# Reducing 32 keys per tile in two more groups of a position-bias network, and a pair in the last one

## The chip, the cores and the metric

The kernel runs on one core of a Trainium2 chip. The metric is device time in microseconds (us) for one launch, taken as the median over several runs. In the listings PE is the matrix engine, PEld its weight loads, DVE the vector engine, ACT the scalar (activation) engine, POOL the GpSimd engine and SP the engine that only issues transfers. POOL and SP both issue DMA transfers here: SP plain copies, POOL copies that add to what lies at the destination.

## The reference, cut to what matters

The input is `x`, two images of 512 channels and 32 x 32 pixels. Layer 0 is an attention block with deformable keys: 8 heads per image give 16 groups, and each group has 1024 queries (the pixels) and 64 keys (sampled positions). Most of the work is a small network that turns every query-key offset into one bias:

```
pos = grid_q[:, :, None, :] - grid_kv[:, None, :, :]
bias = sign(pos) * log1p(abs(pos))
bias = relu(bias @ cpb_w1 + cpb_b1)      # 2 -> 128
bias = relu(bias @ cpb_w2 + cpb_b2)      # 128 -> 128
bias = bias @ cpb_w3 + cpb_b3            # 128 -> 1
sim = q @ k + bias;  attn = softmax(sim);  out = attn @ v
```

The attention's output goes through `out_w` and is added to `x`; then comes an MLP of 512, 2048 and 512 channels. Layer 1 is ordinary attention over the 1024 pixels with four 512 x 512 projections. Everything is float32.

## The kernel before, in words

**Slots.** The bias network runs in one long loop over 256 slots, `for s in range(NS)`. A slot is 4 keys against all 1024 queries, and 16 slots make a group (`NSL = 16`, `NG = 16`). For each slot DVE builds the first hidden layer `h1` in one custom instruction (`st_layer1`, line 678), two slots ahead and into three buffers. PE multiplies it by the second weights in four quarters `z` of 32 hidden channels each (`st_layer2`, line 695). The four keys lie in four groups of 32 output partitions, so a result is 128 partitions (4 keys x 32 channels) x 1024 queries. ACT applies bias and relu (lines 708 and 710).

**Summing channels without PE.** The third layer is a weighted sum over 128 channels. The kernel sums quarters 0 and 1, and 2 and 3, with two DVE instructions (`st_sum`, line 718). A POOL transfer then adds the second sum to the first (line 720). What is left is `sums[s][1]`: 4 keys x 32 partial channels. Then transfers between partitions shrink it, in levels. A *fold* adds half of a tile's rows to the other half (16 partial channels per key). A *copy* puts the free half of the rows of the next tile beside it, and a *join* adds the other half of that tile. After this one tile carries twice as many keys with half as many rows each. Level 1 makes tiles of 8 keys out of pairs of slots, level 2 tiles of 16 keys out of four slots, level 3 tiles of 32 keys out of eight. Folds and joins are POOL transfers (`add`, line 737), copies are SP transfers (`move`, line 744). `LEVELS` (line 785) lists each level's step, the slot at which it ends, its three moves and how many slots after the tile's first slot each is due; `LAST` (line 790) shortens these delays in the last group. `due` collects them, and each slot issues what is due. `add` chains the POOL transfers with `issue_after`, so POOL's queue has a fixed order, and an instruction that waits holds all that is behind it.

**The projection.** `st_layer3` (line 800) multiplies a group's finished tiles by mask weights (`w3f`, `w3u`), which sum the remaining rows of every key. They are made on POOL in `arrange` from columns of the constant `mask`. Each product writes 32 rows of the group's scores `sim` in PSUM: row block `64 h + 32 i`, with `h` the half of the queries and `i` the half of the group's keys. The products accumulate onto q times k (line 809). `FULL = NS - 3 * NSL = 208` says where level 3 ends: groups 0 to 12 have two tiles of 32 keys and 4 products, issued 27 slots after the group's start. Groups 13 and 14 have four tiles of 16 keys and 8 products, issued 22 slots after it (line 934). Group 15, the last, has three tiles of 16 keys. Slots 252 to 255 stand alone, each with its own product (weights `w3u`), and slot 255 has one more for its second sum: 16 products in all, after the loop.

**Softmax and what follows.** `softmax_steps` (line 836) is a generator: ACT takes `sim` out of PSUM, PE transposes it, DVE takes maxima, ACT exponentiates in eight parts and scales, and for every second group PE transposes back (`pb`, line 880). The loop runs one step per slot in most slots. What is left over runs after the loop. There `project(0, ...)` starts the output projection (PE, line 1029); between its products it runs three steps of the last group's softmax at a time.

**Buffers around it.** The first sum of a slot takes a buffer by its place among eight: `u8` (4 buffers), `uo` (3), `uc` (2), and `u4` (2) for place 4. Tile `x6` is a fifth kind, used for slots 228 and 252 in place of `u4` (line 705). After the loop it serves as the fourth block sum that the projection needs, written there by the last `spread` (lines 945 and 946). The other sums of these blocks, `spread` 0 to 2 and `fold` 0 to 3 on `op0`, are done by DVE in the loop, one every fourth slot after slot `ready`.

Of the kernel before, what the change touches and what calls it, by code (L numbers as in the profile page):

```python
# [8 lines left out]
F32 = mybir.dt.float32  # L9
# [48 lines left out]
def conv_seq_kernel(ctx: ExitStack, tc: tile.TileContext, x, xt, kst, pst, cst, vec, wsm, outw, w1, w2, wl, wlt, brow, out):  # L58
# [25 lines left out]
    w3f = cp.tile([P, 80], F32, name="w3f")  # L84
    w3u = cp.tile([P, 60], F32, name="w3u")
    for w in (w3f, w3u):
        nc.gpsimd.memset(w, 0.0)
# [103 lines left out]
    def op_blocks(b, parts, wsum):  # L191
        v, q = vp[:, b * NCH : b * NCH + NCH, :], qa[:, b]
        w = [v[:, k : k + 2, n : n + 256] for k, n in ((0, 0), (2, 0), (2, 256), (0, 256))]
        x = [q[:, k : k + 2, n : n + 512] for k in (0, 2) for n in (0, 512)]
        return w + [wsum[:, j] for j in range(3)], x + [parts[:, j] for j in range(parts.shape[1])]

# [10 lines left out]
    with tc.tile_pool(name="lp", bufs=2) as lp:  # L207
# [32 lines left out]
        nc.gpsimd.dma_start(out=cs, in_=cst)  # L240
        nc.gpsimd.dma_start(out=pz[:, 0:437], in_=pst)
        nc.gpsimd.dma_start(out=ident, in_=kst)

        def load(b, k, wq=None):
# [20 lines left out]
        w2t, crow, tri, chan, mask = (  # L265
            pz[:, a:b] for a, b in ((0, 128), (128, 256), (256, 384), (384, 385), (385, 437))
        )
# [26 lines left out]
        def arrange():  # L294
# [18 lines left out]
            nc.gpsimd.tensor_scalar(w3f[:, 48:64], mask[:, 32:48], sc[:, 8:9], None, ALU.mult)  # L313
            nc.gpsimd.tensor_scalar(w3u[:, 28:32], mask[:, 48:52], sc[:, 8:9], None, ALU.mult)

        state = {}
# [371 lines left out]
        def st_layer2(s):  # L688
            h1 = h1s.pop(s)
            r = []  # L690
            for z in range(4):
# [10 lines left out]
                )[z]  # L702
                pool = lp
                if z == 1 and s % 8 == 4 and s >= FULL and (s - FULL) // 8 % 3 == 2:
                    pool, name, bufs = op, "x6", 1
                o = pool.tile([P, 2, 512], F32, name=name, bufs=bufs)
                if z % 2 == 0:
# [72 lines left out]
        def st_join3(s):  # L780
            for o, i in zip(fours(s, 1), fours(s + 4, 0)):
                add(o, i)

        FULL = NS - 3 * NSL
        LEVELS = (
            (8, FULL, (st_copy3, st_join3, st_fold3), (14, 15, 11)),
            (4, NS - 4, (st_copy2, st_join2, st_fold2), (7, 8, 6)),
            (2, NS - 4, (st_copy, st_join, st_fold), (3, 4, 2)),
        )
# [10 lines left out]
        def st_layer3(s):  # L800
# [17 lines left out]
            if s + NSL == NS:  # L818

                w = [w3u[:, 12 - 4 * o : 44 - 4 * o] for o in range(4)]  # L820
                parts[1][1:] = [(w[o], sums[s + 12 + o][1]) for o in range(4)] + [(w[3], sums[s + 15][3])]
                parts[0] = 4 * [None] + parts[0]
            for m in range(len(parts[1])):
# [69 lines left out]
        for s in range(NS):  # L893
# [19 lines left out]
            if bg is not None and state.get(len(CHAINS) - 1, 0) is None:  # L913

                bg = None
                php.__exit__(None, None, None)
                opp = tc.tile_pool(name="op", bufs=1, side="right")
                op = opp.__enter__()
                op0 = op_blocks(
                    0, op.tile([P, 2, 2, 512], F32, name="op0x"), op.tile([P, 3, 2, 256], F32, name="op0w")  # L920
                )
                ready = s
            if bg is None and s > ready and (s - ready) % 4 == 0 and (s - ready) // 4 <= 7:
                i = (s - ready) // 4 - 1
                if i < 3:
                    spread(op0[1], (i,))
                else:
                    fold(nc.vector, op0[0], which=(i - 3,))

# [14 lines left out]
        next(tail)  # L944
        op0[1].append(op.tile([P, 2, 512], F32, name="x6", bufs=1))
        spread(op0[1], (3,))

# [556 lines left out]
def _order(np):  # L1504
# [9 lines left out]
    alone = (d // 32)[:, None] == np.arange(4)  # L1514
    return np.concatenate([crow, tri, d[:, None], eight, four, alone], axis=1).astype(np.float32)

# [87 lines left out]
```

## Time and profile before

| what | value |
|---|---|
| median of 3 runs | 2612.42 us (2611.72 to 2614.12) |
| the profiled execution's own time | 2612.25 us |
| its span, first to last instruction | 2610.5 us |
| PE busy, in matmuls | 2597.5 us, 19660 instructions |
| DVE busy | 2303.7 us |
| ACT busy | 1754.3 us |
| POOL busy | 980.6 us |
| second-layer products (line 695) | 1772.0 us, 16384 instructions |
| projection products (line 828) | 168 instructions |
| mean busy share of the DMA engines in the loop | mostly 0.8 to 0.9 in the page's 40 slices |

The span is what the profiler sees, and 1.75 us of the execution lie outside it. A float32 product appears as two PE instructions, so a slot's 32 products are 64. Matmuls overlap, so a group's busy time is read from the start times of its rows. A row of the timeline merges neighbours of one kind: start, duration, engine, line, operation, operands, count. The program's names have lost their numbers, so `u` stands for `u8` and `u4`, and `x` for `x6`.

### The profile page before, as it was taken

To read this page: it belongs to the slowest core of one execution; us is meant where nothing else is said; L and a number is where in the kernel's file an instruction comes from. 1 tells how busy PE (TensorE), PEld (TensorE's weight loads), DVE (VectorE), ACT (ScalarE), POOL (GpSimd) and SP (SyncE) were. 2 spreads that over 40 slices of the span, in tenths; PEclk is the share of its full clock that TensorE was granted. 3 is DMA by queue.
4 is the path that set the end of the run, shared out by engine and by line. 5 is a ranking of instruction groups with operands and counts; after the bars stand their busy time and mean duration, and the time that the engine had idled before them with its cause. 6 is when DMAs were issued, how large, how long until landed. Compare 5 with 4: busy or idle time off the path is not lost.

```text
span 2610.5 us, 49004 instructions
## 1 busy us (share of the span) xinstructions
PE 2597.5 (100%) x19660; PEld 1009.8 (39%) x19660; DVE 2303.7 (88%) x1459; ACT 1754.3 (67%) x2362; POOL 980.6 (38%) x1122
## 2 busy tenths in 40 slices
PE   9999999999999999999999999999999999999999
PEld 3332333333233233223333333332355655646656
DVE  6999999999999999999999999999776587666656
ACT  5887888888888888888788777777733242314041
POOL 1344444444444444444454444333322334200100
PEclk9999999999999999999999999999999999999999
DMA  5889999999998999899999899888777768400202
GB/s 187 173 192 197 194 194 195 195 189 191 200 191 189 188 204 203 175 191 202 191 197 192 186 193 193 176 174 186 153 200 171 147 148 167 91 16 1 73 1 56
DMA packets 177634, 428.27 MB, mean 164 GB/s; under 512 B 30048, under 2 KB 78320, under 8 KB 174720
## 3 DMA queue, kind: packets, MB, share of 16 engines
q0 software_dynamic: 107392, 273.09, 58.4%
q1 hardware_dynamic: 69584, 151.75, 17.5%
q8 instruction: 155, 2.54, 0.4%
q14 instruction: 71, 0.58, 0.1%
q10 hardware_dynamic: 432, 0.31, 0.0%
HBM read 82.16 MB, written 6.55 MB: 34 GB/s over the span
## 4 chain that ended last, share of the span: by engine, by line
PE 96%; DVE 3%; ACT 1%; issue 0%; DMA 0%; DVEq 0%; ACTq 0%
PE ps L695 67%; PE sw L1082 7%; PE sw L1253 7%; PE sw L160 7%; PE sw L1029 2%; PE sw L1351 2%; PE psg L597 1%; PE sim L828 1%; DVE hm L137 1%; PE psx L1329 1%; PE sim L809 0%; PE pt L845 0%; PE pkv L534 0%; PE pb L880 0%; PE psq L333 0%
## 5 line engine op out<-in xcount | busy, mean ns | idle before, releaser
L695 PE MATMUL ps<-h,cw 128*32 128x512 f32 x16384 | 1772.0, 592 | 1.8 <-ACT rx L708 1.0
L678 DVE CUSTOM_DVE_ANT_1 h<-ta,tb 128x4096 f32<-128x4096 f32 (+1 forms) x257 | 1131.3, 4402 | 28.9 <-PE ps L695 24.0
L695 PEld LDWEIGHTS ps<-h,cw 128*32 128x32 f32 x16384 | 527.7, 110 | 1214.0 <-issue 1160.4
L708 ACT ACTIVATE rx<-ps,sc 128x1024 f32<-128x1024 f32 x512 | 568.6, 1111 | 138.4 <-PE ps L695 115.5
L737 POOL DMA_DIRECT2D u<-u x394 | 406.9, 1514 | 2.5 <-issue 2.2
L710 ACT ACTIVATE ub<-ps,sc 128x1024 f32<-128x1024 f32 x256 | 308.4, 1205 | 90.6 <-PE ps L695 90.5
L720 POOL DMA_DIRECT2D uo<-ub x127 | 111.4, 877 | 600.1 <-DVE ub L718 570.0
L718 DVE SCALAR_TENSOR_TENSOR ub<-rx,sc,ub 128x1024 f32<-128x1024 f32 x256 | 327.3, 1278 | 3.1 <-ACT ub L710 3.1
L1082 PE MATMUL sw<-hm,w2t 128*128 128x512 f32 x448 | 194.0, 592 | 0.2 <-DVE hm L125 0.2
L710 ACT ACTIVATE uo<-ps,sc 128x1024 f32<-128x1024 f32 x128 | 154.3, 1205 | 43.9 <-PE ps L695 40.7
L718 DVE SCALAR_TENSOR_TENSOR uo<-rx,sc,uo 128x1024 f32<-128x1024 f32 x128 | 163.7, 1279 | 7.6 <-ACT uo L710 7.0
L737 POOL DMA_DIRECT2D u<-uc x124 | 124.8, 1280 | 17.6 <-DMA u<-uc 15.3
L1082 PEld LDWEIGHTS sw<-hm,w2t 128*128 128x128 f32 x448 | 84.9, 190 | 104.0 <-issue 97.9
L720 POOL DMA_DIRECT2D uc<-ub x64 | 55.4, 866 | 179.9 <-DVE ub L718 147.9
L137 DVE TENSOR_TENSOR hm<-hm,sw 128x512 f32<-128x512 f32 x79 | 57.6, 732 | 73.0 <-PE sw L160 50.6
L720 POOL DMA_DIRECT2D u<-ub x62 | 53.1, 856 | 178.8 <-DVE ub L718 178.8
L737 POOL DMA_DIRECT2D uc<-uc x63 | 107.6, 1708 | 0.0
L737 POOL DMA_DIRECT2D uc<-uo x63 | 102.8, 1632 | 10.6 <-DMA uc<-uo 10.3
L1417 POOL DMA_DIRECT2D xs<-rs x6 | 7.2, 1200 | 259.6 <-DVE rs L137 259.6
L737 POOL DMA_DIRECT2D u<-uo x62 | 84.8, 1368 | 21.6 <-DMA u<-uo 18.4
L658 ACT ACTIVATE ta<-fb,vs 128x512 f32<-128x512 f32 (+1 forms) x65 | 89.1, 1374 | 5.6 <-DMA fb<-fdr 5.6
L710 ACT ACTIVATE uc<-ps,sc 128x1024 f32<-128x1024 f32 x64 | 77.0, 1203 | 21.2 <-PE ps L695 19.3
(306 smaller groups left out, 2648.2 us busy)
## 6 DMA issues: line engine op xcount, KB each, us to landing
uo<-ub POOLq DMA_DIRECT2D x127, 512.0 KB, 5.4
fb<-fdr SPq DMA_DIRECT2D x64, 512.0 KB, 5.7
uc<-ub POOLq DMA_DIRECT2D x64, 512.0 KB, 6.0
u<-ub POOLq DMA_DIRECT2D x62, 512.0 KB, 6.3
uc<-uc POOLq DMA_DIRECT2D x63, 256.0 KB, 8.3
uc<-uo SPq DMA_DIRECT2D x63, 256.0 KB, 3.2
uc<-uo POOLq DMA_DIRECT2D x63, 256.0 KB, 5.7
u<-u POOLq DMA_DIRECT2D x62, 256.0 KB, 6.9
```

Of the source, the lines that this page charges most:

```text
L137: nc.vector.tensor_tensor(out, a, b_, op)
L160: nc.tensor.matmul(bank[:, e, :], w, x, start=(q in (1, 2, 5) and e == k == 0), stop=True, skip_group_check=True,)
L658: nc.scalar.activation(ta.rearrange("p j x -> p x j")[:, :, j0:j1], fb[:, 0, :, j0:j1], AF.Identity, bias=col("cb1"), scale=col("w1x"),)
L678: nc.vector._custom_dve(TENSOR_ADD_SAT, out=h1[:, y : y + step].rearrange("p y t x -> p (y t x)"), in0=a.unsqueeze(1).to_broadcast([P, ste ...
L695: nc.tensor.matmul(ps[32 * q : 32 * q + 32, h, :], cw2[:, 32 * z : 32 * z + 32], h1[:, 16 * h : 16 * h + 16, q, :], start=True, stop=True,)
L708: nc.scalar.activation(o, ps, AF.Relu, bias=sc[:, 4 + z : 5 + z])
L710: nc.scalar.activation(o, ps, AF.Relu, bias=sc[:, 4 + z : 5 + z], scale=sc[:, z : z + 1])
L718: nc.vector.scalar_tensor_tensor(r[1], r[0], sc[:, z : z + 1], r[1], ALU.mult, ALU.add)
L720: nc.gpsimd.dma_start(out=sums[s][1], in_=sums[s][3], accum_op=ALU.add)
L737: nc.gpsimd.dma_start(out=out, in_=in_, accum_op=ALU.add)
L1082: nc.tensor.matmul(ps[:, m, :], w[:, a, k, m * P : (m + 1) * P], x[:, b_, k, :], start=(k == 0), stop=(k == 1),)
L1253: nc.tensor.matmul(ps[:, m, :], w[:, a, k, c + m * P : c + (m + 1) * P], x[b_][:, k, :], start=(k == 0), stop=(k == nk - 1),)
```

## The change

`FULL` moves from slot 208 to slot 240, so that groups 13 and 14 reduce to tiles of 32 keys and are projected like groups 0 to 12, and only the last group keeps tiles of 16 keys. Level 1 now ends at slot 254 instead of 252: slots 252 and 253 are folded, copied and joined as a pair, with mask weights of their own (`w3p`, from 8 new columns of the constant). `x6` goes away. Every slot of place 4 takes `u4`, the projection's fourth block sum gets its place in `op0x`, and its `spread` moves into the loop, ahead of the folds, which come four slots later each.

```diff
-    w3u = cp.tile([P, 60], F32, name="w3u")
-    for w in (w3f, w3u):
+    w3u = cp.tile([P, 36], F32, name="w3u")
+    w3p = cp.tile([P, 32], F32, name="w3p")
+    for w in (w3f, w3u, w3p):
         nc.gpsimd.memset(w, 0.0)
...
+            nc.gpsimd.tensor_scalar(w3p[:, 16:24], mask[:, 52:60], sc[:, 8:9], None, ALU.mult)
...
-                pool = lp
-                if z == 1 and s % 8 == 4 and s >= FULL and (s - FULL) // 8 % 3 == 2:
-                    pool, name, bufs = op, "x6", 1
-                o = pool.tile([P, 2, 512], F32, name=name, bufs=bufs)
+                o = lp.tile([P, 2, 512], F32, name=name, bufs=bufs)
...
-        FULL = NS - 3 * NSL
+        FULL = NS - NSL
         LEVELS = (
             (8, FULL, (st_copy3, st_join3, st_fold3), (14, 15, 11)),
             (4, NS - 4, (st_copy2, st_join2, st_fold2), (7, 8, 6)),
-            (2, NS - 4, (st_copy, st_join, st_fold), (3, 4, 2)),
+            (2, NS - 2, (st_copy, st_join, st_fold), (3, 4, 2)),
         )
...
-                w = [w3u[:, 12 - 4 * o : 44 - 4 * o] for o in range(4)]
-                parts[1][1:] = [(w[o], sums[s + 12 + o][1]) for o in range(4)] + [(w[3], sums[s + 15][3])]
-                parts[0] = 4 * [None] + parts[0]
+                w = [w3u[:, 4 - 4 * o : 36 - 4 * o] for o in range(2)]
+                parts[1][1:] = [(w3p, sums[s + 12][1])] + [(w[o], sums[s + 14 + o][1]) for o in range(2)]
+                parts[1].append((w[1], sums[s + 15][3]))
+                parts[0] = 3 * [None] + parts[0]
...
-                    0, op.tile([P, 2, 2, 512], F32, name="op0x"), op.tile([P, 3, 2, 256], F32, name="op0w")
+                    0, op.tile([P, 3, 2, 512], F32, name="op0x"), op.tile([P, 3, 2, 256], F32, name="op0w")
...
-            if bg is None and s > ready and (s - ready) % 4 == 0 and (s - ready) // 4 <= 7:
+            if bg is None and s > ready and (s - ready) % 4 == 0 and (s - ready) // 4 <= 8:
                 i = (s - ready) // 4 - 1
-                if i < 3:
+                if i < 4:
                     spread(op0[1], (i,))
                 else:
-                    fold(nc.vector, op0[0], which=(i - 3,))
+                    fold(nc.vector, op0[0], which=(i - 4,))
...
-        op0[1].append(op.tile([P, 2, 512], F32, name="x6", bufs=1))
-        spread(op0[1], (3,))
...
+    two = (4 * (d % 2) + d // 32)[:, None] == np.arange(8)
-    return np.concatenate([crow, tri, d[:, None], eight, four, alone], axis=1).astype(np.float32)
+    return np.concatenate([crow, tri, d[:, None], eight, four, alone, two], axis=1).astype(np.float32)
```

More of the change, by code (lines that the diff above doesn't have):

```diff
@@ L194, in op_blocks @@
         x = [q[:, k : k + 2, n : n + 512] for k in (0, 2) for n in (0, 512)]
-        return w + [wsum[:, j] for j in range(3)], x + [parts[:, j] for j in range(parts.shape[1])]
+        return w + [wsum[:, j] for j in range(3)], x + [parts[:, j] for j in range(3)]
     zp = ctx.enter_context(tc.tile_pool(name="zp", bufs=3, space=PSUM))
@@ L240, in conv_seq_kernel @@
         nc.gpsimd.dma_start(out=cs, in_=cst)
-        nc.gpsimd.dma_start(out=pz[:, 0:437], in_=pst)
+        nc.gpsimd.dma_start(out=pz[:, 0:445], in_=pst)
         nc.gpsimd.dma_start(out=ident, in_=kst)
@@ L265, in conv_seq_kernel @@
         w2t, crow, tri, chan, mask = (
-            pz[:, a:b] for a, b in ((0, 128), (128, 256), (256, 384), (384, 385), (385, 437))
+            pz[:, a:b] for a, b in ((0, 128), (128, 256), (256, 384), (384, 385), (385, 445))
         )
```

## The prediction

> **What bounds the kernel now.** I read the page's first part, then the chain of work that ended last, in order of time.
>
> ```profile
> PE 2597.5 (100%) x19660; PEld 1009.8 (39%) x19660; DVE 2303.7 (88%) x1459; ACT 1754.3 (67%) x2362; POOL 980.6 (38%) x1122
> 1511.69 0.86 PE sim L828 x8
> 1624.16 1.00 PE sim L828 x8
> 1701.85 1.72 PE sim L828 x16
> 1815.90 1.85 PE sim L828 x16
> 1881.44 4.29 PE sim L828 x25
> ```
>
> From 1480 us to the loop's end the chain never leaves PE, and a slot's 64 matmuls take 6.87 us. So PE sets the end, and every product removed from it is time, unless something makes PE wait. The five rows are the projections of groups 11, 12 (two tiles of 32 keys), 13, 14 (four tiles of 16) and 15.
>
> Next, the timeline of PE at the loop's end, and that of POOL, whose queue feeds it:
>
> ```profile
> 1881.26 1.04 PE L828 MATMUL sim<-u,w3f 128*32 128x512 f32 x4
> 1882.12 1.04 PE L828 MATMUL sim<-x,w3u 128*32 128x512 f32 x4
> 1882.98 0.61 PE L828 MATMUL sim<-uo,w3u 128*32 128x512 f32 x2
> 1885.66 1.13 PE L1029 MATMUL sw<-qa,vp 128*128 128x512 f32 x2
> 1901.12 1.04 PE L880 MATMUL pb<-ident,sx 128*128 128x128 f32 x8
> ```
>
> ```profile
> 1866.10 0.88 POOL L720 DMA_DIRECT2D x<-ub  x1 [3.42 <-DVE ub L718]
> 1868.17 0.84 POOL L737 DMA_DIRECT2D uc<-uo  x1 [1.20 <-DMA uc<-uo]
> 1869.86 0.88 POOL L720 DMA_DIRECT2D uo<-ub  x1 [0.85 <-DVE ub L718]
> 1870.43 1.16 POOL L737 DMA_DIRECT2D u<-uc  x1
> 1877.06 0.82 POOL L737 DMA_DIRECT2D u<-uc  x1 [5.47 <-DMA u<-uc]
> 1877.60 1.17 POOL L720 DMA_DIRECT2D uc<-ub  x1
> ```
>
> PE goes from the last slot into the last projection with no gap: slot 252's own sum (`x`) was started at 1866.10 and is used at 1882.12. The DMA view of these moments gives issue to landing: 5.8 us for `x<-ub` (512 KB), 5.7 for `uo<-ub`, 4.9 for `uc<-uo` (256 KB), 4.8 for the last `uc<-ub`.
>
> [...] 16 instructions over all four row blocks take 1.72 us, while a tile of the last group that fills only two blocks takes 0.86 us for 4 (1882.12 to 1882.98), twice as much each. [...] POOL stood 5.47 us before the join at 1877.06, with slot 254's sum behind it.
>
> **The change part by part**, against the profiled execution (2612.25 us: span 2610.5 and 1.75 around it, 0.17 below the median 2612.42).
>
> 1. Groups 13 and 14 lose four products each. By the chain's rows: 1.72 - 0.86 and 1.85 - 1.00, so -1.71 us, all on PE's path.
> 2. Group 15 loses one two-block tile (two products): -0.86.
> 3. Pair 252/253, the wait added. It is worked out in the clock of before, as both sides move together with PE. The fold can start when 252's sum has landed, 1866.10 + 5.8 = 1871.9. In POOL's new order it stands behind 253's sum and ahead of the first `u<-uc`. It lands behind 253's sum (1875.6), with the 4.9 of a 256 KB row at about 1876.8. The copy then goes out on SP, which is free; SP's copy at 1865.32 let POOL go on at 1868.17, 2.85 us, so 1879.7. The join is last in POOL's queue, behind 254's sum: 1879.7 + 4.9 = 1884.6. PE comes to the pair's product at 1882.12, the second of its order, and everything behind it on PE waits too: the other tiles, the transposes and the projection. **+2.5 us.** Bounds: with the fastest 256 KB landing near the end (4.2) for fold and join the sum is there at 1883.2 (+1.1). With 5.7 for both and 4.85 for the copy (SP 1810.33 to POOL 1815.18) it is 1888.2 (+6.1). I take the middle rows, which carry the load of this moment.
> 4. Softmax of group 14. Its projection moves from 22 to 27 slots after the group's start, group 13's from 230 to 235, and group 13's steps (one more now) fill the slots to 255. So all of group 14's softmax but the read of `sim` falls after the loop; before, all of it but the last scalings was done there. The PE transposes only move (0.59). But ACT now has eight exponentials (2.6 us, as at 1894.11 to 1896.8), eight scalings (2.0) and a copy (0.58) in front of the last group's. It reached these at 1894.11, 6.3 us after taking `sim` at 1887.83. In the new order the first maxima also stand behind the 1.23 us block sum that waits for the last projection. Adding up, `sim` taken at S lets group 14's exponentials end at S+4.2, the projection's copy at 5.2, scalings at 7.2, copy 7.8, maxima 9, exponentials 11.7, then a reciprocal queued behind two PSUM sums, scalings done near S+15. PE reaches `pb` 13.3 after S (1887.83 to 1901.12) and can run one further product within it. **+0.8 us**, between 0 (PE's own delay covers it) and 2.
> 5. The `spread` (1.22 us of DVE at 1883.19) leaves the end, where DVE idled 2.48 before it and PE didn't need it: 0. In the loop it adds 1.2 us to DVE's lag. Counting back 57 tiles `h` from slot 255, the one ready at 1470.3 is used by PE at 1476.8, so 6.5 us cover it: 0. Without cover, 1.2.
> 6. Forty-eight more 64 KB transfers (4 folds, 4 copies, 4 joins for each of 208, 216, 224, 232), 32 on POOL at about 0.54 each, 17 us spread over 40 slots, where POOL is 40% busy and groups 0 to 12 have the same pattern without a PE gap: 0. SP's 16 copies stand ahead of level-2 copies; slot 247's next sum isn't due until 1830.60. Without cover, at most 2.
> 7. POOL's start: one more memset (0.15) and scaling (0.30, the row of `w3u`) before `sc` is finished at 28.5; ACT first needs it at 41.91: 0.
>
> Sum: -1.71 - 0.86 + 2.5 + 0.8 = **+0.7**, 2613.0 for the profiled execution, **2613.1** for the median.
>
> **The rivals.** *The pair arrives in time.* Then -2.57 + 0.4 = -2.2, 2610.2. For it: transfers near the end are few, and 128 KB took 2.6 us at 1877.06. Against: three transfers one after the other in 10.2 us (1871.9 to 1882.12), and no three rows here add to so little (4.2 + 2.85 + 4.2 = 11.3).
>
> *The end is slower by more than 0.2%* (5.2 us; that is about what a measurement of this kernel can tell from no change). One mechanism: the join lands late. It decides from 7.0 us of waiting on (-2.57 + 7.0 + 0.8 = 5.2), a join at 1889.1. Three landings of 5.8 after 1871.9 give 1889.3, 7.2 us, and 2617.8. For it: the copy took 4.85 once. Against: at that time less is in flight than in the loop.
>
> *ACT becomes the bound after the loop.* The `pb` transposes wait 3 us instead of 0.8: +2.9, 2615.3. For it: about 5.2 us of ACT work is new there; before, ACT finished scaling at 1899.16, 2 us before PE needed it. Against: PE's wait for the pair shifts PE as well.
>
> *The transfers of part 6 or DVE's lag reach PE in the loop:* +1 to +3 more, 2615.
>
> **How the numbers follow.** The likeliest (2612 to 2615): 0.56. Pair in time: 0.14. ACT bound: 0.11. Loop stalls: 0.06. Slow join: 0.09. A gain over 5.2 us has no mechanism here, since no more than 2.57 us of PE work is removed: 0.04. The slower chance is the slow join and a small part of the loop stalls. Faster 0.04, same 0.86, slower 0.10. The range 2609.8 to 2617.0 holds the cases but the slow join's upper part.
>
> **What would show it.** Projection rows of 8 instructions for groups 13 and 14 (0.86 to 1.0 us); a PE gap of 1 to 6 us before the pair's product, released by the transfer `u<-uo`; a gap below 2 us before the last `pb`, released by ACT; nothing else idle on PE in the loop. The prediction fails if that first gap is missing or beyond 7 us, or if ACT or DVE hold PE inside slots 208 to 255.

## The result, and the profile after

The changed kernel takes 2617.10 us in the median (14 runs, 2614.41 to 2622.92). The kernel before, run beside it, takes 2612.49 (14 runs, 2611.62 to 2614.12). The ratio is 1.0018, with an interval of 1.0010 to 1.0026. So the change costs some 4.6 us, where +0.7 was forecast and 2617.0 was the upper end of the range. The spread is new too: 8.5 us against 2.5.

The profiled execution of after took 2615.69 us (span 2613.8). It lies at the low end of its runs, 3.4 us above the one of before. The first part of its page shows nothing of this:

```profile
PE 2597.1 (99%) x19640; PEld 1009.2 (39%) x19640; DVE 2299.9 (88%) x1459; ACT 1755.2 (67%) x2362; POOL 1005.3 (38%) x1158
```

PE has 20 matmul records fewer and 0.4 us less busy time; POOL has 36 instructions and 25 us more. The chain of work that ended last, in order of time, shows what happened (start, duration, engine and tile):

```profile
1737.49 0.86 PE sim L828 x8
...
1759.53 35.87 PE ps L697 x333
1795.40 5.34 DMA u<-uo
...
1837.21 4.51 DMA uc<-uo
...
1879.66 5.29 DMA u<-uo
1885.19 4.06 PE sim L828 x18
...
1894.02 5.42 DMA xs<-in_x
```

Before, this chain never left PE between 1480 us and the loop's end. Now it leaves PE at 1795.40, some twelve slots before the end of the loop, and runs for 90 us through POOL, SP and their transfers. Group 13's projection is 0.86 us, as forecast. But what sets the end of the loop is no longer PE's work. It is the time at which the last group's tiles are put together.

PE's timeline at the loop's end (start, duration, instruction, and in brackets the idle time before it with what ended it):

```profile
1880.10 1.05 PE L828 MATMUL sim<-u,w3f 128*32 128x512 f32 x4 [0.52 <-DMA u<-uc]
1885.19 1.07 PE L828 MATMUL sim<-u,w3p 128*32 128x512 f32 x2 [4.04 <-DMA u<-uo]
...
1899.53 7.10 PE L1027 MATMUL sw<-op0x,op0w 128*128 128x512 f32 x16 [1.20 <-DMA xs<-in_x]
```

There are three waits, 5.76 us in all: for the tile of slots 248 to 251, for the pair, and ahead of the output projection's third product. POOL's and SP's timelines show how the pair was built:

```profile
1863.80 0.88 POOL L719 DMA_DIRECT2D u<-ub  x1 [2.24 <-DVE ub L717]
...
1870.03 0.83 POOL L736 DMA_DIRECT2D u<-u  x1 [1.47 <-DMA u<-ub]
...
1877.25 0.81 POOL L736 DMA_DIRECT2D u<-uc  x1 [5.54 <-DMA u<-uc]
1879.09 0.88 POOL L719 DMA_DIRECT2D uc<-ub  x1 [1.02 <-DVE uo L717]
1879.66 1.18 POOL L736 DMA_DIRECT2D u<-uo  x1
```

```profile
1875.82 0.48 SPq L743 DMA_DIRECT2D u<-uo  x1
```

Slot 252's sum (1863.80), its fold (1870.03), the copy on SP (1875.82) and the join (1879.66) are the pair's own steps. The join lands 5.29 us after its issue, at 1884.95. The forecast had 1884.6. But the copy had landed at 1878.04, and the join went out 1.6 us after that. POOL's queue has a fixed order, and the last join of the tile of slots 248 to 251 (1877.25) and slot 254's sum (1879.09) stand ahead of it. The chain of work above comes to the join by way of that tile's moves, not by way of the pair's fold. (For the 1.02 us before slot 254's sum the profile names DVE. That sum follows the join before it by 1.83 to 1.84 us in after and in three more kernels with the pair, where the profile names another releaser twice, so DVE is hardly the cause; what the time goes to isn't shown.)

A fourth loss is in the granted PE clock. The view by stretches has, from left to right, PE's busy time and records, the same for weight loads, DVE, ACT and POOL, then the granted clock, the DMA share and GB/s:

```profile
1882.00:1884.00 2.00, 0.00 (x0) 0.00 (x0) 0.17 (x1) 0.00 (x0) 0.00 (x0) 1.00 1.04 197
1884.00:1886.00 2.00, 0.81 (x3) 0.36 (x6) 0.00 (x0) 0.00 (x0) 0.00 (x0) 0.60 0.19 33
1886.00:1888.00 2.00, 2.00 (x14) 0.75 (x10) 0.00 (x0) 0.00 (x0) 0.00 (x0) 0.54 0.04 8
```

The clock record of the trace has 0.50 from 1884.42 to 1887.83, that is 3.41 us. PE works in 2.6 of these, from 1885.19 on. By an estimate from the granted 0.50, half of that, 1.3 us, is lost.

The sum against before, for the two profiled executions, at the end of the product after `pb` (1910.88 against 1905.43, +5.45): start of the program +0.58, loop -2.30 (two groups' products, 1.71, and group 14's transposes, 0.59, which come back later), group 15's tile -0.86, waits +5.76, half clock +1.3, transposes +0.59. That is +5.1; some 0.4 is not assigned. Afterwards about 2.1 is given back: before, PE waits 1.6 us for DVE's `hm` in four places, and after only 0.2. The other 0.7 I can't place. What remains is 3.3 us of span. The median of after lies another 1.4 us above this execution; what the other executions lose beyond it was not traced.

### The profile page after: what moved, and what is told of

The parts are those of the page before. It is cut to its first block, busy times and chain, and to the rows that moved or that the text cites. A ratio compares the mean times of both kernels' runs of the same rounds, so it can differ in the third digit from the quotient of the medians.

```text
span 2613.8 us, 49094 instructions
## 1 busy us (share of the span) xinstructions
PE 2597.1 (99%) x19640; PEld 1009.2 (39%) x19640; DVE 2299.9 (88%) x1459; ACT 1755.2 (67%) x2362; POOL 1005.3 (38%) x1158
## 4 chain that ended last, share of the span: by engine, by line
PE 88%; DMA 4%; DVE 3%; issue 2%; POOL 1%; ACT 1%; SPq 0%; DVEq 0%; POOLq 0%; ACTq 0%
PE ps L697 59%; PE sw L1080 7%; PE sw L161 7%; PE sw L1251 7%; PE sw L1349 2%; PE sw L1027 2%; DMA u<-uc 1%; PE psg L599 1%; DMA uc<-uc 1%; POOL u L736 1%; DMA uc<-uo 1%; PE sim L828 1%; DMA u<-uo 1%; PE psx L1327 1%; DVE h L680 0%
## 5 line engine op out<-in xcount | busy, mean ns | idle before, releaser
L736 POOL DMA_DIRECT2D u<-u x430 | 439.8, 1512 | 5.9 <-issue 3.4
L709 ACT ACTIVATE u<-ps,sc 128x1024 f32<-128x1024 f32 x64 | 77.1, 1204 | 24.1 <-PE ps L697 20.7
```

Source lines behind the costliest of these rows:

```text
L709: nc.scalar.activation(o, ps, AF.Relu, bias=sc[:, 4 + z : 5 + z], scale=sc[:, z : z + 1])
L736: nc.gpsimd.dma_start(out=out, in_=in_, accum_op=ALU.add)
```

## The experiments

Each kernel was timed beside the kernel before, and "before" is the median of those runs. Three theories were on trial. A: the pair's wait and the slow clock are the loss. B: the softmax of group 14, which now falls behind the loop, is. C: it is the added transfers or a lower clock in the loop. D, E and F refine them as results came in. An "execution" is one of the timed runs of a kernel, and a profile shows one execution of it.

### The two halves of the change apart

The change without the pair:

```diff
-            (2, NS - 2, (st_copy, st_join, st_fold), (3, 4, 2)),
+            (2, NS - 4, (st_copy, st_join, st_fold), (3, 4, 2)),
```

(with the weights and single products of slots 252 to 255 as in before)

> The kernel after without the pair: slots 252 to 255 stand alone again, each with its own product; FULL = 240, u4 and the moved block sum stay. Theory A (the wait for the join, and the slow PE clock after it, is the loss): no wait of 4 us and no slow clock at the loop's end; the product after pb ends about 5.45 - 4.0 - 1.25 + 0.86 = 1 us later than in before, and the median is 2611.5 to 2613, level with before. Theory B (group 14's softmax behind the loop, in ACT's queue ahead of the projection's copy, is the loss): the kernel stays 2 us or more above before, at 2614.5 to 2617. Theory C (the added transfers or a lower granted clock in the loop): slot 255 comes no earlier than in before, and the median stays above 2614.

Measured: 2613.05 against 2612.97, ratio 1.0004 (0.9996 to 1.0013). The profiled execution has no wait for the last tiles, its clock stays at 1.00, and its span is 2609.8, 0.7 below before's. The last projection starts at 1879.53 against 1881.26 in before, and 1.20 us are lost ahead of the third product of the output projection. That is what theory A expects. But the 13 executions fall into two clusters: nine between 2611.17 and 2613.97, four between 2616.40 and 2618.94. Nothing forecast the second one.

The pair alone, on the kernel before:

```diff
-            (2, NS - 4, (st_copy, st_join, st_fold), (3, 4, 2)),
+            (2, NS - 2, (st_copy, st_join, st_fold), (3, 4, 2)),
```

(with `w3p`, its mask columns and the product of the pair; `FULL = 208` and `x6` stay)

> The kernel before with the pair alone: level 1 ends at slot 254, slots 252 and 253 are joined; FULL = 208, tile x6 and group 14's softmax inside the loop as before. Theory A: PE waits 3 to 6 us for the join, the granted PE clock falls to about 0.5 to 0.7 for some 2 us after it, and the median is 2614.5 to 2617.5. Theory B: the wait is there but is absorbed, because ACT's work after the loop is that of before: 2612 to 2613.5.

Measured: 2613.36 against 2612.97, ratio 1.0003 (0.9995 to 1.0011). PE waits 1.97 us for the pair and its clock stays at 1.00. The median lies where theory B has it, though not for B's reason: here the scheduler has put the output projection's first product (2 instructions, 1 us) between the first tile and the pair, so PE comes to the pair later. PE's timeline names no releaser; the join landed at 1885.96:

```profile
1886.06 0.62 PE L831 MATMUL sim<-x,w3p 128*32 128x512 f32 x2 [1.97 <-issue]
```

The halves cost +0.1 and +0.4, the whole +4.6. So they act on each other.

### The order of the last products

The pair's product moved to the end of the list:

```diff
+                parts[1].append(parts[1].pop(1))
```

> The kernel after with the pair's product moved from second to last place among the last group's products, so that the other tiles and, by the scheduler's order, group 14's transposes and the first projection products run while the join is under way. Theory A: the wait of 4.0 us falls to about 1 us or less, PE's clock stays at 1.00, the median falls by 3 to 5 us to 2611.5 to 2613.5. Theory B: the scores of the last group are only complete when the join has landed, ACT takes them later, and the end stays within 1 us of after: 2616 to 2617.5.

Measured: 2614.71, ratio 1.0011 (1.0003 to 1.0019), 2.9 us better than after when each is set against its own before. Part of the loss is thus the pair's place, but theory A's figures are missed: PE now waits 2.63 us for `uc<-ub`, slot 254's own sum, because that sum goes out on POOL at 1879.40, behind the pair's fold and the moves of the tile of slots 248 to 251; in before it went out at 1877.60. The clock still falls to 0.50, for 3.41 us.

Products with zero weights ahead of the pair's product, so that PE isn't idle in the wait. They add nothing to the scores:

```diff
+                for n in range(16 * (s + NSL == NS and m == 1)):
+                    q, t = 64 * (n // 2 % 2) + 32 * (n % 2), parts[1][0][1]
+                    nc.tensor.matmul(sims[gi][q : q + 32, :], w3z, t[:, n // 2 % 2, :], start=False, stop=False)
```

> The kernel after with 16 more products with zero weights (32 instructions over all four row blocks, about 3.4 us at full clock) put on PE just ahead of the pair's product, so that PE is busy while it waits for the join; they add zero to the scores. If the low PE clock after the wait comes from PE standing idle: the clock stays near 1.00, the remaining products and the first projection products take about 2.8 us instead of 4.06, and the median falls by about 1.2 us to 2616. If the low clock has another cause (it came by chance in that execution[...]): it is unchanged, and the median is that of after.

Measured: 2616.74 against 2612.97. The wait fell to 2.05 us, yet the clock went to 0.50 all the same, from 1886.9 to 1890.3. The expected gain of 1.2 isn't there: this kernel is 3.8 us above its before, after was 4.6, and the intervals of the two overlap.

The same with 28 products. In after the clock had fallen 3.27 us after PE went idle (1881.15 to 1884.42), in the kernel above 3.3 us after (1883.6 to 1886.9):

```diff
-                for n in range(16 * (s + NSL == NS and m == 1)):
+                for n in range(28 * (s + NSL == NS and m == 1)):
```

> The kernel after with 28 more products with zero weights (56 instructions, about 6.0 us at full clock) ahead of the pair's product instead of 16, so that PE is busy for the whole wait; they add zero to the scores. If the half clock follows from a stretch of some 3.3 us in which PE was mostly idle: no idle time of over 0.5 us is left there, no slice at 0.50 follows, and the median is about 1.0 to 1.5 us below after's: 2615.5 to 2616.2. If it follows from something else, the slices at 0.50 stay, and the median is 2617 or more.

Measured: 2617.03 against 2612.75; a miss, and on the clock inconclusive. 18 of 21 executions lie between 2615.39 and 2618.30 and three at 2622.98 to 2623.99. The profiled one (span 2621.1) is of the late kind, and it shows what that kind is. PE's waits:

```profile
PE sim L832 <- DMA u<-uc: 6.0, 1, 6.0
```

PE stands at the very first product, ahead of the added ones, for the tile of slots 248 to 251: 6.0 us, where after's profile has 0.52. POOL's and SP's timelines of this execution, and then the same three steps of after:

```profile
1864.09 1.56 POOL L720 DMA_DIRECT2D u<-ub  x1
1873.63 0.84 POOL L737 DMA_DIRECT2D uc<-uo  x1 [7.99 <-DMA uc<-uo]
```

```profile
1867.32 0.47 SPq L744 DMA_DIRECT2D uc<-uo  x1
```

```profile
1866.81 0.84 POOL L736 DMA_DIRECT2D uc<-uo  x1 [2.13 <-DMA uc<-uo]
```

```profile
1863.95 0.47 SPq L743 DMA_DIRECT2D uc<-uo  x1
```

The sum `u<-ub` goes out at about the same time in both (1864.09, 1863.80). The copy on SP goes out 3.2 us after it in the late execution and 0.15 after it in the other. It lands in 5.7 us in the late one and in 2.3 in the other. POOL stands for it, and this join goes out 6.8 us later than in after, the join and the sum behind it 5.4 us later. The copy that went out 3.2 us behind the 512 KB sum (landing 8.3 us after issue) lands 0.7 us after the sum does. In after another copy, at 1837.21, went out 2.9 us behind a sum, took 4.5 us and also landed 0.7 us after it, while the one at 1863.95 landed 3.5 us ahead of its sum (2.3 against 5.9 us from issue). The traces show this order, not what makes it.

### The softmax of group 14

The scheduler takes one softmax step per slot. Without the pair, but with two steps per slot in the last 16 slots, so that group 14's softmax is back inside the loop:

```diff
-                    if next(tails[0], 0) is not None:
-                        tails.pop(0)
+                    for _ in range(2 if s >= NS - NSL else 1):
+                        if tails and next(tails[0], 0) is not None:
+                            tails.pop(0)
```

> The kernel without the pair (FULL = 240, slots 252 to 255 alone) and with two softmax steps per slot in the last 16 slots, so that group 14's softmax is done inside the loop as in before. Theory D (the work of groups 13 and 14 in FULL = 240 gains its 1.7 us, and group 14's softmax behind the loop gives it back, through the wait ahead of the projection's third product, and in some executions 4 to 5 us more): that wait of 1.2 us is gone, the median is 2610.5 to 2611.5, and the executions at 2616 to 2619 are gone. Theory C (the added transfers in the loop cost the time in some executions): the executions at 2616 to 2619 stay, and the median is 2612 to 2613.5.

Measured: 2612.86 against 2612.75. The wait of 1.20 and the cluster at 2616 are gone, as theory D says, but the gain isn't there: ACT takes the scores and PE transposes them in the same slot, so PE waits 1.9 us for ACT's `ss`. A slow clock follows inside the loop, from 1861.92 to 1865.34 (PE's timeline, then the view by stretches):

```profile
1860.46 0.66 PE L844 MATMUL pt<-ident,ss 128*128 128x128 f32 x4 [1.91 <-ACT ss L840]
```

```profile
1862.00:1865.00 3.00, 3.00 (x20) 0.80 (x16) 2.97 (x4) 1.07 (x1) 0.46 (x1) 0.50 0.61 175
```

PE works through all of these 3.41 us, so by an estimate from the granted 0.50 they cost another 1.7.

With the pair in its place, and with the pair last:

> The kernel after (with the pair) and two softmax steps per slot in the last 16 slots. Theory D: with group 14's scores out of the way, projection products of other images come in front of the pair's product as in the kernel with the pair alone, PE stands still for 2 us instead of 4, and the median is 2611 to 2613. If the pair's wait alone sets the loss: 2614.5 to 2616.5, since the join lands no earlier.

> As the last, with the pair's product moved to the end of the last group's products. Theory D: PE's wait falls to about 2 us or less, for slot 254's sum, which stands behind the pair's moves on POOL's queue; 2610.5 to 2612.5. Theory C: 2613 or more, with executions at 2617 and above.

Measured: 2613.52 and 2613.12 against 2612.75 (ratios 1.0005, 0.9997 to 1.0013, and 1.0001, 0.9992 to 1.0009). PE waits 1.9 us for the pair, or 1.2 for slot 254's sum, and 1.9 for `ss` in each. In the first the clock stays at 1.00; in the second it is at 0.50 from 1861.64 to 1865.06, after the wait for `ss`. Between 1480 and 1878 us PE runs 3656 instructions in the second and in the kernel without the pair, and 3672 in the first; at the 1.72 us that 16 take in before, the difference is the 1.7 us estimated above. Two of the 13 executions of the first are above 2618, none of the second is above 2614.31. The pair's wait line, in PE's timeline of the first of them:

```profile
1886.56 0.62 PE L828 MATMUL sim<-u,w3p 128*32 128x512 f32 x2 [1.87 <-DMA u<-uo]
```

The join lands no earlier than in after. PE is merely later by itself, so a wait of its own has swallowed most of the other.

Then one step in slot 252 and three in 254 and 255, without the pair, so that the transposes come a slot after `ss`:

```diff
-                    for _ in range(2 if s >= NS - NSL else 1):
+                    for _ in range({NS - 4: 1, NS - 2: 3, NS - 1: 3}.get(s, 2 if s >= NS - NSL else 1)):
```

> The kernel without the pair, with two softmax steps per slot from slot 240 on, but one in slot 252 and three in 254 and 255, so that PE's transposes of group 14's scores come a slot after ACT takes these, not in the same slot. Against the kernel with two steps in each of these slots the wait of 1.9 us for ss is gone: median 2610.8 to 2611.6, which would beat before. If PE then comes too early for the last group's tiles (theory F), the wait for them takes its place and the median stays 2612 to 2613.

Measured: 2610.49 against 2612.80, ratio 0.9994 (0.9986 to 1.0002). The median is 2.3 us below before and below the forecast 2610.8. Eleven executions lie between 2609.48 and 2612.60 and two at 2616.07 and 2616.91, so the interval still touches 1. It is the best kernel found here. Its chain of work stays on PE through the loop's end:

```profile
1866.50 13.87 PE ps L697 x128
1880.37 4.43 PE sim L827 x26
1884.80 1.06 PE sw L1027 x2
```

The same with the pair prices the pair in the good schedule:

> The kernel after, with its pair, and the softmax steps apart. The pair saves 0.86 us of PE and adds a wait of its own: the join was at 1885 to 1886 in every kernel with the pair, PE comes to the pair's product about 1881.1 or, with the first projection product ahead of it, at 1882 to 1883, so 2 to 4 us, and 1 to 1.7 more if the clock falls: median 2612.5 to 2615. If the pair were free here, 2609.6.

Measured: 2614.47 against 2613.00. So the pair costs 3.8 us there (+1.5 against -2.3). PE waits 3.00 us, and the clock falls afterwards:

```profile
1885.89 0.62 PE L828 MATMUL sim<-u,w3p 128*32 128x512 f32 x2 [3.00 <-DMA u<-uo]
```

This kernel and the one with two steps in every slot have the same order of instructions from the pair's product to the last of group 15: 5.25 us here (1885.89 to 1891.14) and 3.56 at full clock there (1886.56 to 1890.12). The slow clock costs 1.7 us when all of it falls on work.

### What makes the last tiles late

One group instead of two, without the pair, first alone and then with group 14 projected later:

```diff
-        FULL = NS - NSL
+        FULL = NS - 2 * NSL
```

> The kernel after without the pair and with FULL = 224 instead of 240: group 13 alone goes over to tiles of 32 keys, group 14 keeps tiles of 16 and its softmax in the loop. Theory E (the third-level transfers of group 14 stand in the queues of SP and POOL ahead of the last group's, and the last group's tiles land late, by 0.5 us in most executions and by some 6 us in some): POOL stands 1 to 3 us, not 7, at the join of slots 244 to 247's time near 1840, no execution is above 2615, the gain of one group (0.86) is kept, median 2611.5 to 2612.3. If a late landing has another cause, executions above 2616 stay.

> As the last, with group 14 (tiles of 16 keys) projected 27 slots after its start instead of 22, so that its softmax falls behind the loop as in after, without its third-level transfers. Theory E: no executions above 2616; the median is 0 to 1.5 us above that of the last kernel, for the wait of 1.2 us before the projection's third product. Theory F (the softmax in the loop held the loop up and so gave the transfers their time; taken out of it, PE comes too early for them): executions at 2616 to 2619 as with both groups.

Measured: 2622.73 and 2622.99 against 2612.80, ratios 1.0035 and 1.0039; both expectations fail. PE waits 5.8 us for the tile of slots 248 to 251 in the first kernel and 7.4 us for DVE's `h` in the loop in the second. Both are the kernel after with another `FULL`, and it has no `x6`. With tiles of 16 keys in groups 14 and 15, slots 228, 236 and 244 all need a buffer for place 4, and there are only two. Slot 244 then has to wait until group 14 is projected, which fits both waits. On this reading the two runs price that missing buffer (10 us), not the transfers, and in the change it is `FULL = 240` that allows `x6` to go. The kernel that follows keeps `x6` and doesn't have the loss.

The same question asked of the kernel before, where `x6` then serves slot 244:

```diff
-        FULL = NS - 3 * NSL
+        FULL = NS - 2 * NSL
```

> The kernel before with FULL = 224 alone (its x6 then serves slot 244): group 13 takes tiles of 32 keys, group 14 keeps tiles of 16 and its softmax in the loop. Theory E (group 14's third-level transfers delay the last group's): POOL's queue stands as in before from 1830 on, no execution is above 2615, and the gain of one group (0.86 us) is kept: median 2611.6 to 2612.4. Otherwise executions at 2616 to 2619 appear.

Measured: 2612.22 against 2613.00 (ratio 0.9998, 0.9990 to 1.0006), all 13 executions between 2611.27 and 2614.12, within what theory E expects and 0.8 below before, which the interval doesn't tell from nothing. In this kernel group 13 is projected five slots later and group 14's softmax falls behind the loop as in after. PE's timeline shows the wait that this brings:

```profile
1896.40 7.10 PE L1029 MATMUL sw<-op0x,op0w 128*128 128x512 f32 x16 [1.11 <-ACT sx L871]
```

It costs 1.11 in its place, and PE's waits for `hm` are 1.4 us shorter later on. So in this kernel the softmax behind the loop doesn't make the tiles late and costs about nothing in the end.

Group 14's projection alone put off by five slots, on before:

```diff
-            if s % NSL == t % NSL and s >= t and (s - t < FULL) == (t == 27):
+            if s % NSL == t % NSL and s >= t and (s - t < FULL or s - t == NS - 2 * NSL) == (t == 27):
```

> The kernel before with group 14 projected 27 slots after its start instead of 22, so that its softmax falls behind the loop; no transfer is added. Theory E: no late tiles; only the wait of about 1.2 us before the projection's third product: median 2613 to 2614.5, none above 2616. Theory F (without the softmax in the loop PE and DVE run ahead, and the slot sums, started earlier, go ahead of the small copies): POOL waits some 7 us for the copy at about 1842 as in after, PE waits for the tile of slots 248 to 251, and some executions are at 2617 and above.

Measured: 2612.85 against 2613.00; no execution above 2614.11. It does less than I expected of it: ACT takes group 14's scores at 1861.23 as before at 1861.29, since that softmax queues behind group 13's in any case. What moved it in after is group 13's later start. POOL waits 6.27 us for the copy near 1842 here, where before waits 1.20, and yet no tile is late. Theory F had forecast this wait, but with late tiles. So a long wait of POOL's at that place is no mark of the added transfers, as theory E took it to be, nor of late tiles.

The third-level copies and joins of group 14's second tile moved two slots later:

```diff
+                    t += 2 * (step == 8 and kind < 2 and a == FULL - 8)
```

> The kernel after without the pair, with the third-level copies and joins of group 14's second tile two slots later (248 and 249 instead of 246 and 247), where SP and POOL have less to do. Theory E: POOL's 7 us of waiting at about 1842 are gone or moved, the last group's tiles are in time in all executions, and the median is 2611.3 to 2612.3. Theory F: executions at 2616 to 2619 stay, median 2612.5 to 2613.5.

Measured: 2617.83 against 2612.80, ratio 1.0019 (1.0012 to 1.0025). The opposite of what I hoped for: 20 of 21 executions are now at 2616.34 or above. POOL's timeline:

```profile
1834.79 4.06 POOL L736 DMA_DIRECT2D u<-u  x4
1845.45 0.86 POOL L736 DMA_DIRECT2D uc<-uo  x1 [6.61 <-DMA uc<-uo]
```

The four joins now go out at 1834.79, and the next first-level join, which after issues at 1842.29, at 1845.45. The tile of slots 248 to 251 costs PE 3.7 us.

The last group's moves ahead of group 14's in the slots where both are due, on the best kernel:

```diff
-                    due.setdefault(a + t, []).append(((kind > 0, late, late * (10 * step - kind)), moves[kind], a))
+                    due.setdefault(a + t, []).append(((kind > 0, not late, late * (10 * step - kind)), moves[kind], a))
```

> The kernel without the pair, with the softmax steps apart, in which the last group's moves go ahead of group 14's in every slot where both are due (242 to 247). Theory E: POOL's waits at 1842 and 1851 shrink, the executions at 2616 of the last kernel go, and the median stays at 2610.2 to 2610.9. If the order of issue within a slot is not what delays them: as the last kernel, with one or two executions of 13 at 2616.

Measured: 2617.05 against 2613.00, ratio 1.0015 (1.0009 to 1.0022), all 21 executions at 2615.11 or above. It fails in the same way: the four joins go out at 1828.90 instead of 1825.21, a later first-level join at 1846.68 instead of 1842.25, and PE waits 3.9 us. Both kernels keep the added transfers, issue them later, and turn the late tile from an exception into the rule.

At last, in slots 241 to 253 the moves ahead of the sum of the slot before. On trial is whether a copy lands late where a 512 KB sum went out shortly ahead of it, as at 1837.21 in after. First on the best kernel, then on the one just described:

```diff
-            if s > 0:
-                st_sum(s - 1, 2)
-            for _, go, a in sorted(due.get(s, ()), key=lambda e: e[0]):
-                go(a)
+            for late in (False, True):
+                if s > 0 and late == (NS - NSL < s < NS - 2):
+                    st_sum(s - 1, 2)
+                if not late:
+                    for _, go, a in sorted(due.get(s, ()), key=lambda e: e[0]):
+                        go(a)
```

> The kernel without the pair, with the softmax steps apart, in which in slots 241 to 253 the moves between partitions go out ahead of the sum of the slot before. If the small copy lands late [...], POOL's waits at the first-level joins (5.8 us near 1842 there) fall to about 3 us, no execution is at 2616, and the median is 2610.0 to 2610.8. If the sums, now behind a waiting join, become late instead, PE waits for the sums of slots 252 to 254 at the loop's end, 1 to 3 us, and the median is 2611.5 to 2613.5.

> The same order in the kernel that puts the last group's moves ahead of group 14's and was late in every execution (2617.05). If the sum ahead of the copy keeps the lateness going: POOL's waits of 8 to 9 us fall to 3 to 4, PE's wait of 3.9 us goes in most executions, median 2610.5 to 2612.5. If the lateness is only the sum of POOL's work in these slots, whatever its order: 2616 to 2618 as before.

Measured: 2624.56 and 2614.20 against 2613.25. The order decides, but not by the simple rule. In the first kernel the sums themselves become late: POOL waits up to 7.2 us for one before it can fold it, and PE 9.9 us at the loop's end. In the second, 3.1 us are won, each kernel set against its own before, and PE's wait is 2.2 instead of 3.9. No slow clock follows (PE's timeline, then the view by stretches):

```profile
1882.87 1.05 PE L827 MATMUL sim<-u,w3f 128*32 128x512 f32 x4 [2.20 <-issue]
```

```profile
1884.00:1886.00 2.00, 1.64 (x8) 0.29 (x4) 0.00 (x0) 0.00 (x0) 0.00 (x0) 1.00 1.03 197
```

There SP's copy at 1867.26 goes out ahead of the sum (1870.80), and POOL issues the join that needs it at 1870.26, 3.0 us after the copy instead of 6.8 in the kernel without this order. That speaks for the copy and the sum getting in each other's way. What keeps a late queue late isn't settled by it.

## Why the prediction failed, point by point

**Part 1, groups 13 and 14: right.** Their projections took 0.86 and about 1 us, and without the pair the first tile of group 15 came at 1879.53 against 1881.26, in an execution that was 0.71 us later than before's at 1512 us; 0.59 of this gain are group 14's transposes, which come back later. One group alone gained 0.8 of its 0.86, though that is not clear of the noise.

**Part 2, one tile fewer in group 15:** no run shows it apart from the pair.

**Part 3, the wait for the pair: the step that failed first.** The join was forecast for 1884.6 and landed at 1884.95, though by other steps: sum to fold 6.2 us instead of 5.8, fold to copy 5.8 instead of 4.9, then the join behind slot 254's sum at 1879.66 as forecast. That fold, copy and join come one after the other was the author's estimate. In after's trace they do: the fold goes out at 1870.03 and lands at 1875.7, the copy goes out at 1875.82 and lands at 1878.04, and the join goes out at 1879.66. What failed is the sentence that both sides move together with PE. PE was done with the first tile at 1881.15, about a microsecond sooner than the forecast's 1882.12, by the very gain of part 1 and by group 14's transposes leaving the loop. The pair's chain began sooner too, 2.3 us before the forecast's 1866.10, but from the issue of the sum to the landing of the join it took 21.2 us, where the forecast's rows make 18.5. Each step was longer, and the largest part, 1.0 us, lies between the copy and the join, which stood in POOL's queue behind the tile of slots 248 to 251. That tile's last join went out at 1877.25, in before at 1877.06, although PE left the loop 1.7 us sooner (1879.58 against 1881.26). So what PE saved came back as waiting, and the wait is 4.04, not 2.5. Four kernels with the pair show the same: their joins landed at 1884.95 (after), 1885.65 (steps apart), 1885.96 (pair alone) and 1886.32 (two steps), within 1.4 us, while PE was ready for the pair at 1881.15, 1882.89, 1884.09 and 1884.69. The waits are 4.04, 3.00, 1.97 and 1.87.

**The clock, missing from the sum.** The forecast priced a wait by its length alone. In after, 1.3 us more were lost at half clock by the estimate above, and 1.7 measured in the kernel with the steps apart. In the profiles the waits of 2.05, 2.63, 3.0, 3.7, 3.9, 4.04 and 6.0 us at this place, and two of 1.90 and 1.91 for `ss` in the loop, were followed by 3.41 us at 0.50. Those of 2.20, 1.97, 1.87 and 1.20 here, and a third for `ss` of 1.91, weren't.

**Part 6, 48 added transfers at nothing: by the signs wrong, and then the second failed step.** The late executions point here. With group 13's transfers alone there are none (2611.27 to 2614.12). With group 14's added there are 4 of 13, with the softmax steps apart 2 of 13, and issuing group 14's third-level joins 3.7 to 9.4 us later makes nearly all late. The forecast averaged 17 us of issuing over 40 slots and leaned on groups 0 to 12, which have the same pattern. But the group after group 14 is the last: its delays are shortened, its tiles are needed at once, and in the late traces POOL's queue isn't caught up by the end of the loop. The transfers alone don't make a tile late: with two softmax steps per slot and no pair they are all there, PE comes later, and none of 13 executions is above 2614.74. Whether the transfers or PE's sooner arrival is the cause, the runs don't separate. That the four late executions without the pair are of the kind traced in the kernel with 28 products is inferred from their size; none of them was traced.

The 0.52 ahead of the first tile belongs to the pair rather than to these transfers. Without the pair they are there too, and PE doesn't wait for that tile in the trace. The tile's last copy takes 4.56 us to land in after, and 3.31 and 3.26 in the traces of the change without the pair and of the kernel with the steps apart.

**Part 4, group 14's softmax behind the loop, +0.8: near in size, wrong in place.** The wait came ahead of the output projection's third product (1.1 to 1.2 us), not at `pb`. The profile names ACT's scalings for it in the kernel with one group, and the load `xs<-in_x` in after. The times point to neither. In after, in the change without the pair and in the kernel with one group and `x6`, PE starts 0.1 to 0.2 us after two DVE additions (in after line 1035, ending at 1899.32), which read the first product and follow ACT's copy of it. In after that copy (1896.88) stands directly behind group 14's exponentials; in before it ran at 1890.58, and PE didn't wait. The kernels whose softmax is back in the loop don't have the wait. So ACT's queue holds PE as the forecast described, by "the projection's copy", but at another product. The loss is given back later by shorter waits for `hm`.

**Parts 5 and 7, at nothing:** no profile shows a PE wait there.

**The rivals.** The slow join was to decide from 7.0 us of waiting and give 2617.8. The pair waited 4.04, but in the profiled execution all waits and the slow clock together came to 7.1, and the median came to 2617.1. So a loss of the size it priced was there, reached by three shorter waits and a clock instead of one late join. That the figures meet is chance: in that execution 2.1 us are given back. The rival of transfers reaching PE (2615, at 0.06) was given far too little. ACT as the bound did not happen.

**What stays open:** why the change's halves cost 0.1 and 0.4 and the whole 4.6. Most of the 4.1 us between is seen: with the pair alone the loop ends later and one product of the output projection stands in front of the pair, so PE waits 1.97 instead of 4.04 and keeps its clock, which is 2.1 and 1.3 us. It is also open what makes a tile late in some executions, and why products with zero weights in the gap gained nothing measurable.

## What to carry to other kernels

When an engine is the bound but its inputs at the end come through a serial chain of transfers, work the chain out in its own time, with all that stands ahead of it in its queues, and don't let it move with the engine: here what PE saved turned into waiting at the end. Count the clock with a wait on PE: of the seven waits between 1.87 and 2.20 us here three were followed by a stretch of 3.41 us at half clock, and every longer one at the loop's end by one at least. By the estimate above that cost 1.3 us in after, and 1.7 were measured in the kernel with the steps apart. Before adding transfers to a queue with a fixed order, like POOL's here, look at the deadline of the last tile, not at the mean load.

## What was unexpected of the hardware

After's clock record has 1877.33 us at full clock, 3.41 at half and 723.63 at full, that is 550, 1 and 212 times 3.413 us; before's has 2604.37 at full, 763 times. (Both have a last stretch at half at the kernel's very end.) Nine profiles have one stretch of 3.41 us at half ahead of the end. In the three with waits of 5.8, 7.4 and 9.9 us the mean clock of the execution is lower, 0.998 against 0.999, and after the 5.8 and the 9.9 PE runs at half for some 5 us: its first four instructions take 1.92 us there, 1.03 to 1.05 at full clock.

The length of a wait doesn't decide alone: 1.90, 1.91 and 2.05 us were followed by a slow stretch, and 1.87, 1.91, 1.97 and 2.20 us were not. What decides isn't shown by these runs. The fall came 2.8 to 5.2 us after PE went idle (2.84 with the pair last, 3.27 in after, 5.24 with 28 products), so behind a short wait it hit work that was already running again.

In after, a copy of 256 KB on SP took 2.3 us to land where it went out 0.15 us behind a 512 KB POOL transfer, and 4.5 where it went out 2.9 us behind one. In three late traces it took 5.7 to 6.2 us at 2.3 to 3.2 us behind one.
